# Layer 1 of a two-layer transformer block: output projection fenced behind the next scores, its addition behind the copies, and the first feed-forward input made beside the attention

## The chip, the cores and the metric

The kernel runs on one NeuronCore of one Trainium2 chip (trn2). The metric is device time in microseconds: the median of several runs. Beside it stands one execution taken with the hardware profiler, from which all rows of the trace are read.

The engines are called as the profile calls them: PE (TensorE) multiplies matrices, and PEld is its weight load; DVE (VectorE) and ACT (ScalarE) do elementwise work and read PSUM, the memory into which PE writes; POOL (GpSimd) does elementwise work on SBUF only; SP issues transfers. Each engine executes its own queue in order.

## The reference

Two layers run one after the other over 2048 tokens of 512 channels. Layer 0 has a windowed attention and a mixture of experts; the change leaves them as they are. Layer 1 is, in short:

```python
h = layernorm(x) * (1 + ca) + sa
x = x + ga * attention(h)      # 16 heads of 32, 4 key heads, window 128, 16 leading tokens always seen
h = layernorm(x) * (1 + cb) + sb
x = x + gb * ffn(h)

def attention(h):
    q, k, v = rope(h @ Wq + bq), rope(k of h @ Wkv + bkv), v of h @ Wkv + bkv
    return softmax(q @ k.T / sqrt(32), masked) @ v @ Wo + bo

def ffn(h):
    h = fwht(h * SU_ug) / 64
    h = silu(h @ W_gate.T * s_gate) * (h @ W_up.T * s_up)
    h = fwht(h * SU_dp) / 64
    return h @ W_down.T * s_down
```

`fwht` is the normalised Walsh-Hadamard transform over the last axis: 512 for the input, 2048 for the second. Everything is float32.

## The kernel before, in words

The 2048 tokens are 16 tiles of 128 rows; `x_sb` holds them all in SBUF through the whole kernel. The code is one program in Python that unrolls every loop. It states an order of instructions; a planner then writes the queue of each engine. The planner walks through the program in a timeline of its own, with estimated durations: an engine that is free takes, of the instructions that it believes ready, the one that stands earliest in the code. So an instruction from far below can be pulled ahead into a gap (the statistics `st_f`, `mv_f` of the feed-forward input are done tile by tile within the attention), and two instructions can come out in another order than the code has them. The real durations play no part in that order; semaphores see to it that it is safe. `tc.issue_after(ins)` fixes one thing: instructions made in its block stand behind `ins` in the queue of its engine. It makes no engine wait for another.

A buffer is a tile of a pool: tiles of one tag share `bufs` places, and a tile has to wait until its place is free. A pool that is opened after another was closed uses the same space again, and its first writers wait for the last readers of the old tiles.

**Layer 1's attention** (pools from L1052 on). Its work is cut in units `(i, jp)`: tile `i` and half of the heads, 32 units. `scores(i, jp)` makes 32 small matmuls into four PSUM banks (tag `s`, `bufs=4`, so one unit fills all four); for each of its eight head groups DVE reduces the scores with mask and maximum (`ng`, `nb`, L1096) and ACT makes the exponentials with their sum (`pr`, L1106). Keys for a tile are gathered by POOL (`kw`, L1062). `turn(i, jp)` transposes the probabilities on PE (`pt`, L1124, two banks with tag `t`, four transposes to a bank) and copies them to SBUF (`pts`, L1125), on DVE for the first 128 keys and on ACT for the others. `values(i)` multiplies by the values (`o`), spreads the reciprocal sums over the channels by 16 small products (`rd`), and DVE makes `oTs` from both (L1151, L1152). `out1(i)` multiplies by `wo` (`po`, eight matmuls of 512 columns; it uses the same PSUM bank as `rd`) and returns the addition to `x_sb` (L1159) as a step for later.

The loop runs over step `a`: the scores of unit `a`; the addition that is waiting; `values` of the tile whose second half was unit `a-2`; `turn` of unit `a-1`; and at once `out1` of that tile. So the projection is in the code ahead of the scores of step `a+1`, and its addition behind them.

**The feed-forward part** (from L1178). Opening its pools places the weights `wug` (64 KB a partition) and `wd` in the space that the attention used; 16 transfers of 512 KB for `wug`, on SP and ACT in turns, and four of 1 MB for `wd` follow (L1186, L1188). `ffn_in(g)` makes the input of four tiles: statistics, `xn_f` (L229), transposes `nT_f` (L243), their eviction with scale and shift into `hT` (L245 on ACT, L247 on DVE), two stages of butterflies over the four chunks of channels (L1200, L1201: on DVE for `g = 0`, on POOL for the others), and a product with the 128x128 Hadamard matrix (`xh`), copied out by ACT (L1207). Then, for each of 16 chunks `f` of the inner channels, come `gate` and `up` (eight matmuls of 512 columns each), SiLU on ACT (`sg`, L1229), the product on DVE (`act`, L1231), and `y` for the chunk before. `gate` and `up` have one PSUM bank each.

All matmuls carry line L129, which is the helper `mm`; they are told apart by tile name.

Of the kernel before, what the change touches and what calls it, by code (L numbers as in the profile page):

```python
# [22 lines left out]
P = 128  # L23
T = 2048
NT = T // P
D = 512
# [97 lines left out]
def block_kernel(ctx: ExitStack, tc: tile.TileContext, t: dict, out: bass.AP):  # L124
# [90 lines left out]

    def normed(tiles, pool, tag):
        n = len(tiles)
        mv = small.tile([P, n, 2], F32, tag="mv", name=f"mv_{tag}_{tiles[0]}")
        for a, i in enumerate(tiles):
            st = small.tile([P, 6], F32, tag="st", name=f"st_{tag}_{i}")  # L220
            V.bn_stats(st, x_sb[:, i, :])
            V.bn_aggr(mv[:, a, :], st)
        rs = small.tile([P, n], F32, tag="rs", name=f"rs_{tag}_{tiles[0]}")
        S.activation(rs, mv[:, :, 1], AF.Sqrt, bias=eps)
        V.reciprocal(rs, rs)
        got = []
        for a, i in enumerate(tiles):
            xn = pool.tile([P, D], F32, tag="xn", name=f"xn_{tag}_{i}")
            V.tensor_scalar(xn, x_sb[:, i, :], mv[:, a, 0:1], rs[:, a : a + 1], ALU.subtract, ALU.mult)  # L229
            got.append(xn)  # L230
        return got

    def normed_T(tiles, hT, c0, scale, shift, pool, psum, tag, ptag="ps", keep=None):
# [6 lines left out]
        for c in range(KC):  # L240
# [5 lines left out]
            else:  # L246
                V.tensor_scalar(hT[:, c, c0 : c0 + n], ps[:, :n], scale[:, c : c + 1], shift[:, c : c + 1], ALU.mult, ALU.add)  # L247

    modp = ctx.enter_context(tc.tile_pool(name="modp", bufs=1))
# [234 lines left out]
    su_dp = load(l1, "L1_su_dp", [P, FC])  # L484
    ws_dp = load_row(l1, "L1_ws_dp", D)
    bo1 = load_row(l1, "L1_bo", D)
# [485 lines left out]
    with tc.tile_pool(name="a1", bufs=1) as ap:  # L972
# [10 lines left out]
        with tc.tile_pool(name="b1", bufs=1) as bp, tc.tile_pool(name="b1h", bufs=2) as hp, tc.tile_pool(  # L983
# [8 lines left out]
            for g in range(NT // 4):  # L992
# [51 lines left out]
                if g == 0:  # L1044
                    nc.sync.dma_start(
                        out=v2[64:80, :, :, :].rearrange("p i a m -> p (i a) m"), in_=bc(va[0:16, 0, :], 1, 2 * NT)
                    )

        with tc.tile_pool(name="s1", bufs=2) as sp, tc.tile_pool(name="q_s", bufs=4, space=PSUM) as p_s, tc.tile_pool(
            name="q_t", bufs=2, space=PSUM  # L1050
# [3 lines left out]
            W = P + 64  # L1054
            keys, prs, pts_, outs, totals = {}, {}, {}, {}, {}

# [9 lines left out]
            def scores(i, jp):  # L1066
# [9 lines left out]
                for cp in range(2):  # L1076
# [3 lines left out]
                    for c2 in range(2):  # L1080
                        for a in range(2):
                            for j, s in ss.items():
                                r = slice(32 * j, 32 * j + 32)
                                q0 = i * P + 64 * a
                                mm(
                                    s[64 * a : 64 * a + 64, c2, 0:nk],
# [3 lines left out]
                    for c2 in range(2):  # L1090
                        for j, s in ss.items():
                            c = 2 * cp + c2

                            nb = small.tile([P, 1], F32, tag="nb", name=f"nb_{i}_{c}_{j}", bufs=6)
                            ng = sp.tile([P, W + 16], F32, tag="ng", name=f"ng_{i}_{c}_{j}", bufs=4)
                            V.tensor_tensor_reduce(  # L1096
# [17 lines left out]
            def turn(i, jp):  # L1114
# [3 lines left out]
                for j in (2 * jp, 2 * jp + 1):  # L1118
                    pr = prs.pop((i, j))
                    for b in range(1 if i == 0 else 2):  # L1120
                        n = 80 if b else P
                        pt = p_t.tile([P, 4, P], F32, tag="t", name=f"pt1_{i}_{j}_{b}")
                        for c in range(4):
                            TE.transpose(pt[0:n, c, :], pr[:, c, b * P : b * P + n], ident)  # L1124
                        (S.copy if b else V.tensor_copy)(  # L1125
                            pts_[i][0:n, b, j, :], pt[0:n].rearrange("p c q -> p (c q)")
                        )

            def values(i):
# [17 lines left out]
                for c in range(4):  # L1147
                    for j in range(4):
                        mm(rd[32 * j : 32 * j + 32, c, :], rs[:, c, j : j + 1].to_broadcast([P, HD]), ident)
                outs[i] = sp.tile([P, 4, P], F32, tag="oTs", name=f"oTs_{i}")  # L1150
                S.copy(outs[i], o)  # L1151
                V.tensor_tensor(outs[i], outs[i], rd, ALU.mult)  # L1152

            def out1(i):
# [4 lines left out]
                return lambda: V.tensor_tensor(x_sb[:, i, :], x_sb[:, i, :], po, ALU.add)  # L1159

            units = [(i, jp) for i in range(NT) for jp in range(2)]
            add = None
            for a in range(len(units) + 3):
                if a < len(units):
                    scores(*units[a])
                if add is not None:
                    add()
                    add = None
                done = units[a - 2][0] if 2 <= a < len(units) + 2 and units[a - 2][1] == 1 else None
                if done is not None:  # L1170
                    values(done)
                if 1 <= a <= len(units):
                    turn(*units[a - 1])
                if done is not None:
                    add = out1(done)


    with tc.tile_pool(name="f1", bufs=1) as fp, tc.tile_pool(name="f1n", bufs=5) as np_, tc.tile_pool(  # L1178
# [11 lines left out]
        def ffn_in(g):  # L1190
            hT = hp.tile([P, KC, D], F32, tag="hT", name=f"hT2_{g}", bufs=1)
            normed_T(list(range(4 * g, 4 * g + 4)), hT, 0, sc, sh, np_, p_t, "f1")
            xh = hp.tile([P, KC, D], F32, tag="xh", name=f"xh_{g}")
            src, dst = hT, xh
            h = 1
            while h < KC:
                a = src.rearrange("p (n two h) m -> p n two (h m)", two=2, h=h)
                b = dst.rearrange("p (n two h) m -> p n two (h m)", two=2, h=h)
                eng = G if g else V
                eng.tensor_tensor(b[:, :, 0, :], a[:, :, 0, :], a[:, :, 1, :], ALU.add)  # L1200
                eng.tensor_tensor(b[:, :, 1, :], a[:, :, 0, :], a[:, :, 1, :], ALU.subtract)  # L1201
                src, dst = dst, src
                h *= 2
            for c in range(KC):
                ps = p_t.tile([P, D], F32, tag="ps", name=f"xh_{g}_{c}")
                mm(ps, had, src[:, c, :])
                S.copy(xh[:, c, :], ps)  # L1207
            return xh

        xh = ffn_in(0)  # L1210
        for g in range(NT // 4):
# [95 lines left out]
```

## Time and profile before

| what | us |
|---|---|
| median of 3 runs (2305.62 to 2310.59) | 2306.02 |
| the profiled execution's own time | 2301.6 |
| its span (first to last instruction) | 2299.8 |
| PE busy in the span | 2122.3 |
| PE weight loads | 1178.8 |
| DVE busy | 847.7 |
| ACT busy | 473.6 |
| POOL busy | 559.0 |
| layer 1: end of the first output projection | 1331.3 |
| layer 1: end of the last output projection | 1578.0 |
| layer 1: start of the first gate matmul | 1601.5 |

Busy times are sums over the whole span and hide stages with different limits, and the ends of matmuls are modelled, so that a busy PE need not be doing all that it could. A row of the trace's groups reads "line, engine, operation, output <- inputs, shapes, count | busy us, mean ns of one | idle time ahead of it and what ended it". A row of waits reads "waiting engine, tile and line <- what ended the wait: us in total, times, longest". The chain is the work that ended last, followed back from the end: each piece with its start, its duration, engine, tile and line.

### The profile page before, as it was taken

To read this page: it belongs to the slowest core of one execution; us is meant where nothing else is said; L and a number is where in the kernel's file an instruction comes from. 1 tells how busy PE (TensorE), PEld (TensorE's weight loads), DVE (VectorE), ACT (ScalarE), POOL (GpSimd) and SP (SyncE) were. 2 spreads that over 40 slices of the span, in tenths; PEclk is the share of its full clock that TensorE was granted. 3 is DMA by queue.
4 is the path that set the end of the run, shared out by engine and by line. 5 is a ranking of instruction groups with operands and counts; after the bars stand their busy time and mean duration, and the time that the engine had idled before them with its cause. 6 is when DMAs were issued, how large, how long until landed. Compare 5 with 4: busy or idle time off the path is not lost.

```text
span 2299.8 us, 27707 instructions
## 1 busy us (share of the span) xinstructions
PE 2122.3 (92%) x10584; PEld 1178.8 (51%) x10584; DVE 847.7 (37%) x2177; ACT 473.6 (21%) x1114; POOL 559.0 (24%) x444
## 2 busy tenths in 40 slices
PE   3999978999999999999639999997999999999999
PEld 3665645545555566676315555554444444444444
DVE  3246655154544433345366456554011011000101
ACT  0124413111111111111001356653010010010000
POOL 2300000365665666654424100000010010010000
PEclk9899975799999999999869899998999999999999
DMA  9800113589899899999752000005000000000000
GB/s 355 299 2 19 38 58 110 166 200 224 220 236 235 208 244 239 253 301 313 163 195 59 19 2 1 2 2 218 2 0 19 0 0 4 15 0 0 19 0 19
DMA packets 137350, 256.40 MB, mean 111 GB/s; under 512 B 52649, under 2 KB 55657, under 8 KB 134657
## 3 DMA queue, kind: packets, MB, share of 16 engines
q1 hardware_dynamic: 95136, 159.48, 20.9%
q0 software_dynamic: 36032, 77.30, 16.2%
q10 hardware_dynamic: 6048, 17.83, 2.1%
q8 instruction: 85, 1.39, 0.2%
q14 instruction: 49, 0.39, 0.1%
HBM read 180.56 MB, written 71.65 MB: 110 GB/s over the span
## 4 chain that ended last, share of the span: by engine, by line
PE 81%; DVE 6%; DMA 6%; ACT 4%; issue 1%; POOL 1%; ACTq 0%; POOLq 0%; SPq 0%; DVEq 0%
PE y L129 18%; PE gu L129 10%; PE up L129 9%; PE gate L129 9%; PE gub L129 5%; PE xp L734 3%; PE q L129 3%; ACT pr L1106 3%; PE s L129 3%; PE po L129 2%; PE mod L129 2%; PE po_a L129 2%; DMA sum<-yo,tidx 2%; PE o L129 2%; PE pt L1124 2%; PE tps L129 2%
## 5 line engine op out<-in xcount | busy, mean ns | idle before, releaser
L793 POOL DMA_INDIRECT sum<-yo,tidx x164 | 268.7, 1638 | 120.6 <-DMA sum<-yo,tidx 36.5
L507 POOL DMA_INDIRECT xring<-h_d,tidx x164 | 168.0, 1025 | 510.9 <-DVE tidx L687 331.3
L1231 DVE SCALAR_TENSOR_TENSOR act<-up,L_ws_up,sg 128x512 f32<-128x512 f32 x64 | 48.1, 751 | 598.6 <-PE up L129 598.6
L129 PE MATMUL gu<-xT,w 128*128 128x312 f32 (+26 forms) x1024 | 245.5, 398 | 6.6 <-DVE xT L739 6.6
L129 PE MATMUL gate<-xh,wug 128*128 128x512 f32 x512 | 230.7, 592 | 0.0
L129 PE MATMUL up<-xh,wug 128*128 128x512 f32 x512 | 230.7, 592 | 0.0
L129 PE MATMUL y<-wd,act 128*128 128x512 f32 x512 | 229.5, 592 | 0.0
L129 PEld LDWEIGHTS gu<-xT,w 128*128 128x128 f32 x1024 | 191.7, 192 | 60.7 <-issue 16.5
L1229 ACT ACTIVATE sg<-gate,L_ws_gate 128x512 f32<-128x512 f32 x64 | 44.0, 687 | 575.4 <-PE gate L129 575.4
L129 PEld LDWEIGHTS up<-xh,wug 128*128 128x128 f32 x512 | 97.3, 190 | 122.5 <-issue 122.5
L129 PEld LDWEIGHTS y<-wd,act 128*128 128x128 f32 x512 | 97.3, 190 | 122.5 <-issue 122.5
L129 PEld LDWEIGHTS gate<-xh,wug 128*128 128x128 f32 x512 | 96.8, 190 | 119.6 <-issue 119.6
L129 PE MATMUL y<-w,hA 128*128 128x512 f32 (+22 forms) x328 | 148.8, 596 | 0.9 <-DVE yo L789 0.9
L789 DVE SCALAR_TENSOR_TENSOR yo<-y,wc,modr 128x512 f32<-128x512 f32 (+22 forms) x164 | 117.1, 745 | 80.1 <-PE y L129 68.4
L737 ACT ACTIVATE xT<-xp,modc,modc 128x312 f32<-128x312 f32 (+26 forms) x128 | 74.3, 580 | 316.0 <-PE xp L734 286.3
L1200 POOL TENSOR_TENSOR xh<-hT 128x1024 f32<-128x1024 f32 x3 | 7.6, 2524 | 503.3 <-DVE xn_f L229 335.9
L1106 ACT ACTIVATE pr<-ng,nb 128x208 f32<-128x208 f32 (+1 forms) x256 | 115.4, 453 | 55.1 <-DVE nb L1096 55.1
L129 PE MATMUL gub<-xT,w 128*64 128x312 f32 (+26 forms) x1024 | 125.4, 398 | 0.0
L734 PEld LDWEIGHTS xp<-cst,xring 128*128 128x128 f32 x656 | 72.3, 141 | 68.1 <-issue 46.6
L734 PE MATMUL xp<-cst,xring 128*128 128x128 f32 x656 | 98.3, 282 | 1.9 <-DVE xT L739 1.2
L755 DVE TENSOR_TENSOR hA<-hA,gu 128x312 f32<-128x312 f32 (+26 forms) x64 | 28.2, 440 | 186.7 <-PE xp L734 99.6
L129 PEld LDWEIGHTS gub<-xT,w 128*64 128x64 f32 x1024 | 70.5, 137 | 44.8 <-issue 11.3
(311 smaller groups left out, 2662.6 us busy)
## 6 DMA issues: line engine op xcount, KB each, us to landing
w<-in_L_gu SPq DMA_DIRECT2D x64, 768.0 KB, 7.3
sum<-xring SPq DMA_DIRECT2D x5, 4352.0 KB, 21.9
w<-in_L_dn SPq DMA_DIRECT2D x64, 256.0 KB, 8.3
wm<-in_L_wmod SPq DMA_DIRECT2D x9, 1024.0 KB, 6.8
w<-in_L_dn SPq DMA_DIRECT2D x64, 128.0 KB, 8.7
sa<-sum SPq DMA_DIRECT2D x32, 256.0 KB, 9.0
h_d<-xn_f SPq DMA_DIRECT2D x16, 256.0 KB, 2.9
wda<-in_L_Wdown SPq DMA_DIRECT2D x8, 512.0 KB, 13.9
```

The lines of the kernel that those rows point to most:

```text
L129: return TE.matmul(o, lhsT, rhs, start=start, stop=stop)
L507: return G.indirect_dma_start(out=dst, out_offset=None, in_=src[:, :], in_offset=bass.IndirectOffsetOnAxis(ap=idx, axis=0))
L734: st_["pe"] = TE.transpose(xp[:, b * P : (b + 1) * P], xg[:, c * P : (c + 1) * P], ident)
L737: S.activation(xT[:, c, 0:n], xp[:, 0:n], AF.Identity, bias=sh, scale=sc)
L755: V.tensor_tensor(o[:, 0:n], o[:, 0:n], ps[1][:, 0:n], ALU.mult)
L789: V.scalar_tensor_tensor(yo, ys[h], shares[h][rows, b : b + 1], m0[5][rows, :], ALU.mult, ALU.mult)
L793: G.indirect_dma_start(out=sums[k][:, :], out_offset=bass.IndirectOffsetOnAxis(ap=idx, axis=0), in_=yo, in_offset=None, compute_op=ALU.add,)
L1106: S.activation(prs[i, j][:, c, :nk], ng[:, :nk], AF.Exp, bias=nb, scale=-1.0, accum_out=totals[i][:, c, j : j + 1],)
L1124: TE.transpose(pt[0:n, c, :], pr[:, c, b * P : b * P + n], ident)
L1200: eng.tensor_tensor(b[:, :, 0, :], a[:, :, 0, :], a[:, :, 1, :], ALU.add)
L1229: S.activation(sg, pg, AF.Silu, scale=wsg[:, f : f + 1])
L1231: V.scalar_tensor_tensor(acts[f], pu, wsu[:, f : f + 1], sg, ALU.mult, ALU.mult)
```

## The change

- In step `a` of the attention's loop the projection no longer follows `turn`. It is written one step later, behind the scores of that step, and fenced on PE behind the last score matmul (`behind["PE"]`). Its addition is written behind `turn` of that later step, fenced on DVE behind the last copy of transposed probabilities there (`behind["DVE"]`).
- The input of the first four tiles of the feed-forward part (`hT0`, `xh0`) is made in a generator `ahead()`. From step 16 on, one piece of it follows each step: the statistics; one tile at a time its `xn`, its transposes into one bank of tag `t` and four evictions of 128x128; the butterflies, on POOL; two empty pieces; and one Hadamard product with its copy at a time. Its tiles lie in a pool `fx` of their own on the other side of SBUF. The feed-forward part then starts with `xh0`.
- To make room, `ng` has three buffers in place of four, `oTs` one in place of two, and the row `ws_dp` lies in a pool that is closed before layer 1.
- The butterflies become a function, always on POOL; `normed` is cut in two (`moments` and the rest).

```diff
-    def normed(tiles, pool, tag):
+    def moments(tiles, tag):
         n = len(tiles)
...
         V.reciprocal(rs, rs)
+        return mv, rs
+
+    def normed(tiles, pool, tag):
+        mv, rs = moments(tiles, tag)
...
+    def butterflies(eng, src, dst):
+
+        h = 1
+        while h < KC:
+            a = src.rearrange("p (n two h) m -> p n two (h m)", two=2, h=h)
+            b = dst.rearrange("p (n two h) m -> p n two (h m)", two=2, h=h)
+            eng.tensor_tensor(b[:, :, 0, :], a[:, :, 0, :], a[:, :, 1, :], ALU.add)
+            eng.tensor_tensor(b[:, :, 1, :], a[:, :, 0, :], a[:, :, 1, :], ALU.subtract)
+            src, dst = dst, src
+            h *= 2
...
-    ws_dp = load_row(l1, "L1_ws_dp", D)
+    ws_dp = load_row(rp, "L1_ws_dp", D)
...
+        fx = ctx.enter_context(tc.tile_pool(name="fx", bufs=1, side="right"))
...
-                                mm(
+                                behind["PE"] = mm(
                                     s[64 * a : 64 * a + 64, c2, 0:nk],
...
-                            ng = sp.tile([P, W + 16], F32, tag="ng", name=f"ng_{i}_{c}_{j}", bufs=4)
+                            ng = sp.tile([P, W + 16], F32, tag="ng", name=f"ng_{i}_{c}_{j}", bufs=3)
...
-                        (S.copy if b else V.tensor_copy)(
+                        copied = (S.copy if b else V.tensor_copy)(
                             pts_[i][0:n, b, j, :], pt[0:n].rearrange("p c q -> p (c q)")
                         )
+                        if b == 0:
+                            behind["DVE"] = copied
...
-                outs[i] = sp.tile([P, 4, P], F32, tag="oTs", name=f"oTs_{i}")
+                outs[i] = sp.tile([P, 4, P], F32, tag="oTs", name=f"oTs_{i}", bufs=1)
...
+            hT0 = fx.tile([P, KC, D], F32, tag="hT", name="hT2_0")
+            xh0 = fx.tile([P, KC, D], F32, tag="xh", name="xh_0")
+
+            def ahead():
+                mv, rs = moments([0, 1, 2, 3], "f1")
+                yield
+                for i in range(4):
+                    xn = fx.tile([P, D], F32, tag="xn", name=f"xn_f1_{i}")
+                    V.tensor_scalar(xn, x_sb[:, i, :], mv[:, i, 0:1], rs[:, i : i + 1], ALU.subtract, ALU.mult)
+                    ps = p_t.tile([P, KC, P], F32, tag="t", name=f"nT_f1_{i}")
+                    for c in range(KC):
+                        TE.transpose(ps[:, c, :], xn[:, c * P : (c + 1) * P], ident)
+                    for c in range(KC):
+                        o = hT0[:, c, i * P : (i + 1) * P]
+                        if c % 2:
+                            S.activation(o, ps[:, c, :], AF.Identity, bias=sh[:, c : c + 1], scale=sc[:, c : c + 1])
+                        else:
+                            V.tensor_scalar(o, ps[:, c, :], sc[:, c : c + 1], sh[:, c : c + 1], ALU.mult, ALU.add)
+                    yield
+                butterflies(G, hT0, xh0)
+                yield
+                yield
+                for c in range(KC):
+                    ps = p_t.tile([P, D], F32, tag="t", name=f"xh_0_{c}")
+                    mm(ps, had, hT0[:, c, :])
+                    S.copy(xh0[:, c, :], ps)
+                    yield
+
             units = [(i, jp) for i in range(NT) for jp in range(2)]
-            add = None
+            pending = None
+            side = ahead()
             for a in range(len(units) + 3):
                 if a < len(units):
                     scores(*units[a])
-                if add is not None:
-                    add()
-                    add = None
+
+                add = None
+                if pending is not None:
+                    with tc.issue_after(behind["PE"].ins):
+                        add = out1(pending)
+                    pending = None
                 done = units[a - 2][0] if 2 <= a < len(units) + 2 and units[a - 2][1] == 1 else None
                 if done is not None:
                     values(done)
+                    pending = done
                 if 1 <= a <= len(units):
                     turn(*units[a - 1])
-                if done is not None:
-                    add = out1(done)
+                if add is not None:
+                    with tc.issue_after(behind["DVE"].ins):
+                        add()
+                if a >= 16:
+                    next(side, None)
+            for _ in side:
+                pass
...
-            hT = hp.tile([P, KC, D], F32, tag="hT", name=f"hT2_{g}", bufs=1)
+            hT = fx.tile([P, KC, D], F32, tag="hT", name=f"hT2_{g}")
...
-            xh = hp.tile([P, KC, D], F32, tag="xh", name=f"xh_{g}")
...
-                eng = G if g else V
...
+            xh = (hp if g % 2 else fx).tile([P, KC, D], F32, tag="xh", name=f"xh_{g}", bufs=1)
+            butterflies(G, hT, xh)
...
-        xh = ffn_in(0)
+        xh = xh0
```

More of the change, by code (lines that the diff above doesn't have):

```diff
@@ L1054, in block_kernel @@
             W = P + 64
-            keys, prs, pts_, outs, totals = {}, {}, {}, {}, {}
+            keys, prs, pts_, outs, totals, behind = {}, {}, {}, {}, {}, {}
             def window(i):
@@ L1190, in ffn_in @@
         def ffn_in(g):
-            hT = hp.tile([P, KC, D], F32, tag="hT", name=f"hT2_{g}", bufs=1)
+            hT = fx.tile([P, KC, D], F32, tag="hT", name=f"hT2_{g}")
             normed_T(list(range(4 * g, 4 * g + 4)), hT, 0, sc, sh, np_, p_t, "f1")
-            xh = hp.tile([P, KC, D], F32, tag="xh", name=f"xh_{g}")
[L1194 to L1198, printed above, removed]
-                eng = G if g else V
[L1200 to L1203, printed above, removed]
+            xh = (hp if g % 2 else fx).tile([P, KC, D], F32, tag="xh", name=f"xh_{g}", bufs=1)
+            butterflies(G, hT, xh)
             for c in range(KC):
                 ps = p_t.tile([P, D], F32, tag="ps", name=f"xh_{g}_{c}")
-                mm(ps, had, src[:, c, :])
+                mm(ps, had, hT[:, c, :])
                 S.copy(xh[:, c, :], ps)
             return xh
-        xh = ffn_in(0)
+        xh = xh0
         for g in range(NT // 4):
```

## The prediction

> **What bounds the kernel now.** The page comes first: PE is busy 92% of the span and holds 81% of the chain that ended last. That average hides the two places that the change touches, so next comes the chain in order of time over layer 1's attention. One tile of it:
>
> ```profile
> 1438.22 0.85 PE s L129 x12
> 1439.07 1.87 PE o L129 x32
> 1440.94 0.88 PE rd L129 x32
> 1441.81 1.02 PE pt L1124 x8
> 1443.34 1.03 PE pt L1124 x8
> 1444.36 3.45 PE po L129 x8
> 1447.83 0.70 DVE x_sb L1159
> 1448.56 0.69 DVE st_f L221
> 1450.00 3.35 ACT pr L1106 x15
> ```
>
> The end of a tile hangs together in series: the projection `po` (PE), its addition (DVE), then the statistics, and only behind these the next reductions `ng` and exponentials `pr`. The waits of the same stage (1320 to 1560 us: total, times, longest) say who pays:
>
> ```profile
> ACT pr L1106 <- DVE nb L1096: 52.3, 19, 4.6
> DVE x_sb L1159 <- PE po L129: 40.3, 14, 3.7
> ```
>
> DVE stands with the addition at the head of its queue until `po` has ended; the reductions behind it wait, and ACT behind them. Afterwards PE pays: from the end of `po` to the first `o` (1447.8 to 1455.8) it has only 60 scores and 16 transposes, 5.4 us of work, in 8.0 us. A table of windows (span, busy PE, PEld, DVE, ACT, POOL, clock, DMA) shows a whole stage, an ordinary tile, and one in three times a slower one:
>
> ```profile
> 1331.30:1567.70 236.40, 225.59 (x2344) 138.26 (x2345) 141.44 (x577) 148.32 (x527) 9.52 (x36) 0.96 0.01 2
> 1415.30:1431.50 16.20, 15.52 (x170) 9.77 (x167) 9.94 (x41) 9.93 (x37) 0.79 (x3) 1.00 0.01 2
> 1447.80:1467.00 19.20, 18.52 (x170) 10.60 (x171) 10.14 (x42) 11.74 (x39) 0.79 (x3) 0.82 0.01 2
> ```
>
> From the end of the first `po` to that of the fifteenth are 14 tiles, 16.89 us each. DVE and ACT need about 10 us of that; neither is a bound. PE's busy 15.5 is no measure, as matmul ends are modelled, so I add its work from rows where it runs dense: 64 scores at 0.0555 (28 in 1.55 us) 3.55, 32 transposes at 0.128 4.08, `o` 1.87, `rd` 0.88, `po` 3.45: 13.8 us. The tile at clock 0.82 ran `o` and `rd` in 5.2 us instead of 2.8, right after the quiet 8 us; three of the 14 did, some 9 us in all.
>
> The second place is the boundary to the feed-forward part, in the chain from 1574 us:
>
> ```profile
> 1574.29 3.71 PE po L129 x8
> ...
> 1578.92 10.49 DMA wug<-in_L_Wug
> 1589.41 0.02 issue
> 1589.43 0.34 ACTq L1186
> 1589.77 0.05 issue
> 1589.82 1.46 ACT hT L245 x2
> 1591.30 1.23 DVE xh L1200
> ...
> 1595.06 6.47 PE xh L129 x8
> ```
>
> The last `po` ends at 1578.0, the first `gate` starts at 1601.5: 23.5 us with 5.5 us of PE work. Its longest piece is no need for data: ACT issues eight weight transfers, stalls in them until 1589.8, and the evictions `hT` stand behind.
>
> **The change, part by part.**
>
> *Projection behind the next scores, addition behind the copies.* Nothing is removed. PE's order in a pair of units becomes: scores, `po`, 16 transposes | scores, `o`, `rd`, 16 transposes, or 7.3 and 6.6 us, where it was 3.8 and 10.0. An ACT half is eight `pr` at 0.45 plus two or three copies at 0.57, at most 5.3 us, and fits under either. Behind the fenced `po` stand 16 transposes on PE; their `pr` were done a unit earlier. Behind the fenced addition stand the next reductions on DVE, delayed by 0.7 us under 3 us of PE work. The period's floor is 13.8. Transposes have two banks, which opens 0.5 us between pairs (1442.84, now filled by four scores): 14.8 if unfilled, and I add 0.2 for waits. Taken: 15.0; ends 14.2 and 16.9 (the planner orders by its own estimates, so the gain may fail). (16.89 - 15.0) x 14 = **-26.4 us**.
>
> The skill rule that bears on the slow tiles is in "TensorE: Matmul & The Clock Gate", Part 1: an idle window of about 3.4 us halves PE's clock. The row: 0.82 after a sparse stretch that is never idle so long. By the rule as worded the sparse stretch is harmless, the slow tiles have another cause and stay (-18); by the row, which links them to sparseness, they go with it (-26). I go by the row.
>
> *Shorter buffers.* `ng` 4 to 3: DVE makes one in 0.295 us, ACT takes one in 0.45, so ACT never lacks one; DVE's last reduction of a unit ends one ACT step, 0.45, later, hidden under `po` or `o`. Without that cover it costs 0.9 a tile, 12.6 us. `oTs` 2 to 1 and `ws_dp`'s other pool: nothing, since `po` of the tile before has ended half a tile earlier, and the row is loaded in the same place of SP's queue.
>
> *The first feed-forward input beside the attention.* Moved: the statistics and the root with its two 1.28 us table loads, which already stand in the attention (the planner had pulled them ahead); 4 `xn` (0.54 on DVE); 16 transposes; their evictions, now 16 of 128x128 in place of 4 of 128x512; 4 butterflies, from DVE (1.22 each) to POOL; 8 `xh` matmuls; 4 copies (0.59 on ACT). No DMA is issued or passed. On a PE that sets the pace: 16 x 0.128 + 8 x 0.43 = 5.5 us. Evictions of 128x128 are not in the trace: between 0.17 and 0.37 on DVE (128x4, 128x208 rows), 0.30 and 0.45 on ACT; I take 0.25 and 0.35, near the larger forms, so 0.7 us for a tile with the engines side by side. Each of the eight extra users of the two transpose banks may hold PE up for 0 to 0.9 us; I take 0.4: 3 us. Sum **+8.5**; ends 4 (half of the PE work falls in gaps) and 16 (`xh` placed before POOL is done, as in the feed-forward part: 4.2 us idle and 3.0 at half clock).
>
> Against it speaks "SBUF — State Buffer", "Who interferes with whom": a VectorE instruction in a two-port mode and a GpSimd one exclude each other for a whole instruction. The row:
>
> ```profile
> L229 DVE TENSOR_SCALAR xn_f<-x_sb,mv_f,rs_f x4: 540/1552/2580, 1693.7 to 1697.1; 128x512 f32<-128x512 f32 x4
> ```
>
> Beside POOL's butterflies an `xn` took up to 2.58 us. By the rule alone, DVE work beside 10.1 us of butterflies (4 at 2.52) is at risk; but here the four `xn` come before the butterflies by their data, and the reductions, copies and additions read PSUM or one SBUF operand, which the rule excepts. Taken 0; 5 us at the other end. Key windows on POOL (0.8 us a tile) are made some 20 us early (at 1439.2 for scores at 1462) and stand a 10 us delay.
>
> *The boundary after.* The first transfers issue when the last `po` frees their space, as now, and landed 4.7 to 5.0 us later: `gate` 0 at +4.8, `up` 0, +11.7. `gate` 1 needs `sg` 0, which stands behind ACT's eight issues (+11.8), a table load (1.28) and itself (0.69): +13.8, a stall of 2.1. PE at half clock after its 4.8 us idle (`xh` 6.47 for 3.43) would delay `gate` 0 by up to 3; that overlaps this stall. So 6.9 us instead of 23.5: **-16.6**; ends -13 and -19.
>
> *Sum.* -26.4 + 8.5 - 16.6 = -34.5. The profiled execution took 2301.6 us (span 2299.8); the median of the three runs is 4.4 above it. 2301.6 - 34.5 + 4.4 = **2271.5 us**.
>
> **The rivals.** Each has its time from the same three terms.
>
> (B) *ACT's pace takes the wait's place.* Sixteen `pr` and six copies in the planner's order hold the period at 16.2, and only the slow tiles go: -9.7 + 8.5 - 16.6 gives 2288. For it: DVE's shorter lead and "pts" copies that stand behind eight reductions. Against: ACT is busy under 10 us in 16.2.
>
> (C) *PE saturated, side work in gaps.* Period 14.2, side work at 5: -37.7 + 5 - 16.6 gives 2257. For it: ACT and DVE have 4 us to spare. Against: table loads and two transpose banks.
>
> (D) *Slower.* `po` and `rd` share one PSUM bank. If the copies, with the addition fenced behind them, end up behind the next unit's reductions on DVE, `rd` waits for the addition: 3.45 us of `po` stay in series and 0.8 (0.69 and the handover) come on top each tile, period 17.7: +11.3 + 8.5 - 16.6 gives 2309. It decides from 0.6 us a tile ((16.6 - 8.5) / 14) upward. Against: the copies need only transposes that PE runs before the next scores.
>
> (E) *The fences change nothing* because the planner ends up where it was, and side work meets a full PE: terms cancel only by accident.
>
> **How the numbers follow.** Chances: forecast 0.55, B 0.22, C 0.12, D 0.09, E 0.02. The forecast's own range is 2261 to 2284 (period 14.5 to 15.5, and 4 us from the rest). For 8 in 10 the range reaches into C and through most of B: **2255 to 2298**, leaving out D, E and C's lower part. Under 0.2% (4.6 us) this kernel's change can't be told from none. Forecast, B and C are faster: 0.89; same 0.02; slower 0.09.
>
> **What would show it.** Right: the addition no longer waits for `po`; ACT's wait for `nb` falls from 52 us to under 25; tiles at 15.0 us with the clock at 1.00; side matmuls at about half of the attention; first `gate` 5 us after the last `po`, `gate` 1 waiting for `sg`. Wrong: tiles still over 16 us with ACT or PSUM banks in the waits (B), `rd` waiting for `x_sb` (D), or PE idle ahead of `xh` for POOL.

## The result, and the profile after

| | us |
|---|---|
| before, median of 4 runs beside the changed kernel (2301.39 to 2310.59) | 2305.82 |
| changed kernel, median of 4 runs (2273.07 to 2276.15) | 2274.12 |
| ratio, with its 95% interval | 0.9863 [0.9842, 0.9884] |
| changed kernel's profiled execution; its span | 2273.46; 2271.2 |

The kernel became 1.4% faster, 31.7 us between the medians; the forecast was 2271.5. The spans differ by 28.6 us, and a few marks in both traces say where. The marks are the first copy of a gathered key window (POOL, `kw`), the end of the last `po` (read, here and in all that follows, at the start of the addition that waits for it), the start of the second gate (`gate` 1), and the end of the span. A stage is one execution's; the ratio rests on the medians.

| stage | before | after | difference | forecast |
|---|---|---|---|---|
| start of the span to the first key window | 1303.4 | 1306.7 | +3.3 | 0 |
| first key window to the end of the last `po` | 274.6 | 264.7 | -9.9 | -17.9 |
| end of the last `po` to `gate` 1 | 30.2 | 15.6 | -14.6 | -16.6 |
| `gate` 1 to the end | 691.6 | 684.2 | -7.4 | 0 |

So the total came out right, and its terms did not: the attention gave little more than half of what was forecast, and the feed-forward part gave 7.4 us that the forecast did not have (about 1.8 of them are work that moved across the mark; see the second input below). The first row is code that the change leaves alone. Over the 13 profiles of this case its mark lies between 1303.4 and 1312.6, so it is spread between executions.

One tile of the attention after, in the chain in order of time (start, us, engine, tile, line, instructions):

```profile
1413.11 3.63 PE po L129 x8
1416.74 0.87 PE pt L1141 x8
1417.61 0.50 PE s L129 x4
1418.11 1.02 PE pt L1141 x8
1419.13 0.90 PE s L129 x14
1420.54 3.82 ACT pr L1123 x16
1424.35 0.48 ACT oTs L1170
1424.86 0.69 DVE oTs L1171
1425.55 0.61 DVE pts L1142
1426.20 0.63 PE pt L1141 x4
1426.83 1.55 PE s L129 x28
1428.39 3.63 PE po L129 x8
```

`po` is followed at once by transposes; the addition and the statistics are gone from the chain. From `po` to `po` is 15.28 us. What is left of a series lies at the end of the second half: ACT's last exponentials and its copy, then on DVE `oTs`, then `pts`, and only then the transposes that PE needs.

The waits of the same stage (1320 to 1540 us: total, times, longest):

```profile
ACT pr L1123 <- DVE nb L1113: 16.1, 24, 1.7
...
DVE rs L1164 <- ACT pr L1123: 9.9, 11, 1.0
```

In the same window before, ACT waited 47.6 us for the reductions, and DVE 37.0 us with the addition for `po`, which is not in the list any more. (The prediction's 52.3 and 40.3 are of a window 20 us longer.) The second row is not new: DVE stands with the reciprocal of the sums at the head of its queue until ACT has made the last exponential, and before this took 13.1 us in 10 waits. With the addition gone, it is what stands ahead of the copies.

The table of windows (window, its length, busy PE, PEld, DVE, ACT, POOL, granted clock, share of DMA, GB/s) for 14 tiles, the one slow tile, and an ordinary one:

```profile
1336.30:1561.20 224.90, 213.89 (x2347) 131.35 (x2345) 147.40 (x573) 153.07 (x523) 18.80 (x40) 0.98 0.01 2
1384.80:1404.10 19.30, 18.06 (x176) 10.49 (x172) 11.04 (x45) 13.10 (x41) 0.79 (x3) 0.82 0.01 2
...
1413.10:1428.40 15.30, 14.70 (x170) 9.25 (x169) 10.33 (x44) 10.26 (x38) 0.79 (x3) 1.00 0.01 1
```

The 14 tiles took 224.9 us where they took 236.4; six of them now carry side work. The ordinary one is 0.9 us shorter than before (16.2), and one tile at clock 0.82 is left of three.

The boundary after, PE's timeline (start, us, line, operation, tiles, shapes, instructions, and in brackets the idle time ahead and what ended it):

```profile
1567.67 3.70 PE L129 MATMUL po<-L_Wo,oTs 128*128 128x512 f32 x8 [0.85 <-DVE oTs L1171]
1572.70 1.72 PE L247 MATMUL nT_f<-cst,xn_f 128*128 128x128 f32 x8 [1.33 <-DVE xn_f L233]
1576.37 5.40 PE L129 MATMUL gate<-xh,wug 128*128 128x512 f32 x8 [1.96 <-DMA wug<-in_L_Wug]
1581.60 3.60 PE L129 MATMUL up<-xh,wug 128*128 128x512 f32 x8
1585.04 0.60 PE L247 MATMUL nT_f<-cst,xn_f 128*128 128x128 f32 x4
1586.54 0.66 PE L247 MATMUL nT_f<-cst,xn_f 128*128 128x128 f32 x4 [0.91 <-DVE hT L251]
```

The first gate waits for nothing but its weights, 5.0 us after the last `po`. The transposes `nT_f` around it belong to the second feed-forward input (tiles 4 to 7). They were in the middle of the first group's chunks before; the planner has pulled them into this gap.

### The profile page after: what moved, and what is told of

The parts are those of the page before. It is cut to its first block, busy times and chain, and to the rows that moved or that the text cites. A ratio compares the mean times of both kernels' runs of the same rounds, so it can differ in the third digit from the quotient of the medians.

```text
span 2271.2 us, 27760 instructions
## 1 busy us (share of the span) xinstructions
PE 2103.9 (93%) x10584; PEld 1167.8 (51%) x10584; DVE 845.0 (37%) x2179; ACT 479.6 (21%) x1121; POOL 571.4 (25%) x448
## 4 chain that ended last, share of the span: by engine, by line
PE 84%; DVE 6%; DMA 5%; ACT 3%; issue 1%; POOL 1%; ACTq 0%; POOLq 0%; DVEq 0%
PE y L129 19%; PE gu L129 10%; PE gate L129 10%; PE up L129 10%; PE gub L129 5%; PE s L129 4%; PE xp L749 4%; PE q L129 3%; PE po L129 3%; PE mod L129 3%; ACT pr L1123 2%; PE po_a L129 2%; PE pt L1141 2%; PE tps L129 2%; DMA wm<-in_L_wmod 2%; DMA sum<-yo,tidx 1%
## 5 line engine op out<-in xcount | busy, mean ns | idle before, releaser
L129 PEld LDWEIGHTS gu<-xT,w 128*128 128x128 f32 x1024 | 191.4, 191 | 59.3 <-issue 16.7
L1113 DVE CUSTOM_DVE_ANT_0 ng<-s,cst 128x208 f32<-128x208 f32 (+1 forms) x256 | 87.2, 367 | 32.2 <-PE s L129 17.1
```

Source lines behind the costliest of these rows:

```text
L129: return TE.matmul(o, lhsT, rhs, start=start, stop=stop)
L1113: V.tensor_tensor_reduce(out=ng[:, :nk], in0=s[:, c2, :nk], in1=mask, scale=-SCALE, scalar=3e38, op0=ALU.add, op1=ALU.min, accum_out=nb,)
```

## Experiments

The theory to test was the forecast's: three terms, each from its own edit, that add up. The rivals were that the fences do nothing beyond the place in the code, that the shorter buffers cost something, that the slow tiles follow from sparseness alone, and for the 7.4 us in the feed-forward part that they come from the place of the `xh` products and not from the clock. The kernels below ran in three later groups, each with its own runs of the kernel before (medians 2308.56, 2307.92 and 2306.64); a ratio is to those of its own group. All of these kernels compute all that the reference does.

### The projection's new place alone, the side work alone, buffers, fences

The projection and its addition moved, with their fences, on the kernel before:

```diff
+                if pending is not None:
+                    with tc.issue_after(behind["PE"].ins):
+                        add = out1(pending)
...
+                if add is not None:
+                    with tc.issue_after(behind["DVE"].ins):
+                        add()
```

> The kernel before with the projection and its addition moved and fenced alone; buffers as before, no side work, feed-forward input where it was. Theory T (the move takes the projection and its addition out of DVE's and ACT's way; the side work and the boundary are separate terms): an ordinary tile falls from 16.2 to about 15.3 us and slow tiles become fewer, so -16 to -22 us, about 2286; the boundary stays at 23.5 us and the feed-forward part as it was. Rival B (ACT's pace takes the wait's place): at most -6, 2300 or more. Rival D (rd behind the addition): slower than before.

The side work alone is the changed kernel with the loop of before:

```diff
-                    with tc.issue_after(behind["PE"].ins):
-                        add = out1(pending)
+                if add is not None:
+                    add()
...
+                if done is not None:
+                    add = out1(done)
```

> The changed kernel with projection and addition back where they were: the first feed-forward input beside the attention, short buffers, butterflies on POOL. Theory T: the boundary gives about -15 and the second input, which now falls into the boundary, about -7 in the feed-forward part; the side work costs +3 to +9 in the attention: 2287 to 2294. Rival (PE has room in the old order, so the side work is free): 2282 to 2285. Rival (evictions behind the waiting addition stall the transposes): 2298 or more.

The moved projection with the shorter buffers:

```diff
-name=f"ng_{i}_{c}_{j}", bufs=4)
+name=f"ng_{i}_{c}_{j}", bufs=3)
...
-name=f"oTs_{i}")
+name=f"oTs_{i}", bufs=1)
```

> The moved and fenced projection with ng on three and oTs on one buffer, nothing else. Theory T (DVE still leads ACT, and the later last reduction is hidden): the same as the fences alone within 3 us. Rival (without cover, 0.45 us a unit): 6 to 13 us slower than the fences alone.

The changed kernel with everything in its new place and neither fence:

```diff
-                    with tc.issue_after(behind["PE"].ins):
-                        add = out1(pending)
+                    add = out1(pending)
...
-                    with tc.issue_after(behind["DVE"].ins):
-                        add()
+                    add()
```

> The changed kernel with both fences taken out; the projection stays in the code behind the next scores and the addition behind the copies. If the fences carry the gain, the planner puts projection and addition back and it takes 2290 or more. If the place in the code carries it, it is within 4 us of the changed kernel, 2270 to 2278.

Measured, with the stages from the profiles (attention from the first key window to the end of the last `po`, then to the first `up`, then to the end):

| kernel | median us | ratio | attention | to `up` | rest |
|---|---|---|---|---|---|
| before | | | 274.6 | 26.8 | 695.0 |
| changed | 2274.12 | 0.9863 [0.9842, 0.9884] | 264.7 | 10.2 | 689.6 |
| moved, fenced | 2290.65 | 0.9927 [0.9902, 0.9952] | 262.4 | 26.0 | 694.6 |
| side work alone | 2290.25 | 0.9924 [0.9907, 0.9940] | 285.2 | 10.3 | 689.4 |
| moved, short buffers | 2286.74 | 0.9907 [0.9887, 0.9927] | 257.2 | 25.5 | 695.3 |
| changed, no fences | 2271.61 | 0.9838 [0.9820, 0.9855] | 264.3 | 10.2 | 689.5 |

The edits add up. The moved projection changes the attention alone (-12.2, -17.4 with short buffers); the side work costs the attention 10.6 us (3 to 9 were expected) and gives the other two stages 16.5 and 5.6. The two kernels' gains by median, 17.9 and 18.3, sum to 36 us against the changed kernel's 32 to 37 (it was measured again, below).

The shorter buffers cost nothing that shows: the kernel with them is 3.9 us faster than the one without, and the profiles put that on two slow tiles fewer (one in place of three). The fences are not needed for the gain: without them the median is the same within its interval, and PE's queue is nearly the same. It is the place in the code that carries the gain; with the projection behind the scores the planner's own choice comes out almost where the fences would put it. Almost, since an ordinary tile takes 15.72 us without the fences and 15.28 with them. That the attentions come out alike here (264.3 and 264.7 us) is because no tile is slow in the profile without fences and one is in the other.

### The second input's `xh` products

In the trace after, the feed-forward part has three further inputs. Groups of PE's timeline for the second and the third:

```profile
1669.44 3.73 PE L129 MATMUL xh<-hT,cst 128*128 128x512 f32 x8
...
1849.07 2.73 PE L129 MATMUL xh<-hT,cst 128*128 128x512 f32 x4 [4.19 <-POOL hT L259]
1851.99 2.76 PE L129 MATMUL xh<-hT,cst 128*128 128x512 f32 x4 [0.19 <-ACT xh L1256]
```

and the second before:

```profile
1701.95 2.69 PE L129 MATMUL xh<-hT,cst 128*128 128x512 f32 x4 [4.25 <-POOL hT L1200]
1704.88 2.78 PE L129 MATMUL xh<-hT,cst 128*128 128x512 f32 x4 [0.24 <-ACT xh L1207]
```

Before, PE reached `xh` ahead of POOL's butterflies, idled 4.25 us and then ran the products in 5.5 us in place of 3.7. After, the second input was begun at the boundary, its butterflies ran at 1588, and its `xh` finds them done; the third and fourth still wait. If that is the source of the 7.4 us, writing the products four chunks later must give the others the same:

```diff
             butterflies(G, hT, xh)
-            for c in range(KC):
+
+            def rest(after):
+                with tc.issue_after(after.ins):
+                    for c in range(KC):
...
+            return rest
...
                 if f == FC // 2 and g + 1 < NT // 4:
-                    nxt = ffn_in(g + 1)
+                    rest = ffn_in(g + 1)
+                if f == FC // 2 + 4 and g + 1 < NT // 4:
+                    nxt = rest(fed)
```

(`fed` is the last `up` product of that chunk.)

> The changed kernel with the Hadamard products of the later three feed-forward inputs written four chunks later and fenced on PE behind that chunk's last up matmul, so that POOL has time for its butterflies. Theory P (the 7.4 us that the feed-forward part won for its second group are a wait of PE for POOL plus the half clock after it): the third and fourth group win the same, 6 to 7 us each, 12 to 14 in all against the changed kernel, about 2261. Rival (the 7.4 us come from the tiles' new place in memory or from transfers): no change, 2274.

Measured 2257.2 us, 0.9774 [0.9751, 0.9796]. All three inputs look alike now:

```profile
1709.21 3.74 PE L129 MATMUL xh<-hT,cst 128*128 128x512 f32 x8
```

The products at 1879.34 and 2049.46 also take 3.74 with no wait. From the first `up` to the end the kernel needs 676.4 us in place of 689.6: 13.2 for two inputs, 6.6 each. That is what a wait and the slow products behind it cost. (The median fell by 16.9 us where 12 to 14 were expected; no tile of this execution's attention is slow, which makes it 3.5 us shorter.)

The 7.4 us are made of three parts. The second input's wait and products took 4.25 and 5.7 us before and take 3.7 now: 6.2 us, close to the 6.6. Its 16 transposes, about 1.8 us, stood behind `gate` 1 and now stand ahead of it, so that the boundary pays for them: they are moved, not won. And the products of the third and fourth input took 0.7 us more in this execution (12.4 us in place of 11.7).

### DVE's queue at the end of a tile

Where do an ordinary tile's 15.28 us come from, when PE's rows, placed end to end, need 14.4? The queue of DVE around 1425 us after:

```profile
1424.39 0.25 DVE L1164 RECIPROCAL rs<-tot 128x16 f32<-128x16 f32 x1 [0.88 <-ACT pr L1123]
1424.86 0.69 DVE L1171 TENSOR_TENSOR oTs<-oTs,rd 128x512 f32<-128x512 f32 x1 [0.22 <-ACT oTs L1170]
1425.46 1.28 DVE L1142 COPY pts<-pt 128x512 f32<-128x512 f32 x2
```

The copies of the transposed probabilities stand behind two instructions that wait for ACT, and PE's next transposes wait for the copies, 0.9 us with the waits for ACT's copies there. If that is all, putting both instructions behind the copies brings the tile to PE's own sum:

```diff
-                V.reciprocal(rs, totals.pop(i))
+                with tc.issue_after(behind["DVE"].ins):
+                    V.reciprocal(rs, totals.pop(i))
...
-                V.tensor_tensor(outs[i], outs[i], rd, ALU.mult)
+                return lambda: V.tensor_tensor(outs[i], outs[i], rd, ALU.mult)
...
+                if done is not None:
+                    with tc.issue_after(behind["DVE"].ins):
+                        scaled()
```

(The last piece stands behind `turn`.)

> The changed kernel with the scaling oTs fenced on DVE behind the copies of the same step, and the next reciprocal behind the copies of the step before, so that the first copy of transposed probabilities no longer stands behind two waits for ACT. Theory Q (those waits hold the second pair of transposes up by 0.9 us a tile and keep an ordinary tile at 15.3 where PE's rows add up to 14.4): tiles of 14.4 to 14.7, 8 to 12 us faster than the changed kernel, about 2264. Rival (the projection then waits for oTs instead): tiles stay at 15.3 or grow, 2274 or more.

Measured 2268.78 us, 0.9830 [0.9803, 0.9856]. An ordinary tile in its table of windows:

```profile
1412.00:1426.40 14.40, 14.40 (x169) 9.19 (x170) 10.18 (x42) 10.19 (x38) 0.79 (x3) 1.00 0.01 1
```

and DVE's queue there:

```profile
1408.41 0.69 DVE L1142 COPY pts<-pt 128x512 f32<-128x512 f32 x1 [0.52 <-PE pt L1141]
1409.93 0.69 DVE L1142 COPY pts<-pt 128x512 f32<-128x512 f32 x1 [0.83 <-PE pt L1141]
1410.54 0.68 DVE L1172 TENSOR_TENSOR oTs<-oTs,rd 128x512 f32<-128x512 f32 x1
```

The tile is 14.40 us and PE busy for all of it: now DVE waits for PE and no longer PE for DVE. The attention took 254.9 us in place of 264.7; the changed kernel without a slow tile (its repetition, below) took 261.3, so 6.4 of the 9.8 us are the order's. The median fell by only 5.3 us where 8 to 12 were expected, and its interval overlaps the changed kernel's: the tiles show the gain, the total alone would not.

### The clock at the boundary

`gate` 0 took 5.40 us. The table of windows after, two microseconds a row:

```profile
1575.00:1577.00 2.00, 0.63 (x2) 0.39 (x3) 0.94 (x3) 0.00 (x0) 0.00 (x0) 1.00 1.03 428
1577.00:1579.00 2.00, 2.00 (x4) 0.77 (x3) 0.00 (x0) 0.00 (x0) 0.00 (x0) 0.53 1.02 418
1579.00:1581.00 2.00, 2.00 (x4) 0.87 (x3) 0.00 (x0) 0.00 (x0) 0.00 (x0) 0.62 1.02 416
```

In this execution the granted clock falls only after work has come back. (It is not always so: in the kernel of the two edits below it was at 0.50 from 1566.6 us on, 1.2 us before its `gate` 0 began.) Five extra products whose results are overwritten, each counted as two instructions, were to keep PE busy over the gap:

```diff
+                if g == 0 and f == 0:
+                    for k in range(5):
+                        mm(pg, had, xh[:, k % KC, :])
```

> The changed kernel with five extra products (ten matmuls of 512 columns, about 4.3 us) into the first gate bank ahead of the first gate product, whose results the real product overwrites. Theory W (the first gate product takes 5.40 us instead of 3.43 since PE idled at the boundary and its clock fell): it takes 3.43 and the kernel gains 1 to 2 us. Rival (the weights are still landing and slow it): 5.4 as before, no gain. Rival (the extra work delays it): 1 to 3 us slower.

Measured 2276.34 us, 0.9857 [0.9836, 0.9877], the same as without. It decides nothing: six of the ten instructions were placed ahead of the last `po` and four behind it, PE still waited 2.03 us for the weights, and `gate` 0 took 5.30. The three edits together (later `xh`, DVE's order, extra products):

> The three edits of these experiments together on the changed kernel. If their terms are separate, their gains add: 12 to 14 for the later products, 1 to 2 for the warm clock, 8 to 12 for the scaling, about 2250. If they share a cause (the clock), less than two thirds of that, 2257 or more.

Measured 2253.88 us, 0.9758 [0.9740, 0.9776], 20.2 us below the changed kernel where the three expectations add up to 21 to 28. Four of the extra instructions stand behind the last `po` here too, with a wait as long as before, but this time the clock held, and the gates show what the forecast had been looking for:

```profile
1571.26 3.70 PE L129 MATMUL gate<-xh,wug 128*128 128x512 f32 x8 [2.20 <-DMA wug<-in_L_Wug]
...
1580.98 3.70 PE L129 MATMUL gate<-xh,wug 128*128 128x512 f32 x8 [0.59 <-ACT sg L1290]
```

`gate` 0 at full clock, and `gate` 1 waiting for `sg` 0, which stands behind ACT's transfers. Of the 1.7 us won on `gate` 0 about 0.7 are left at `gate` 1 (14.9 us after the last `po` against 15.6). Without the extra products:

> The changed kernel with the later products and the scaling behind the copies, without the extra products at the boundary. If the gains of the two are separate: 2274 - 17 - 6 (their own measured differences), about 2252; if the extra products of the combined kernel were worth their cost, 2256 or more.

Measured 2252.42 us, 0.9755 [0.9740, 0.9769]: the extra products are worth nothing that can be seen, and the gains of the other two edits add up (16.9 and 5.3 by median, 21.7 together).

### Half of the first chunk's weights early

The last wait at the boundary is for weights. The place of `xn` in the pool `fx` is free once the side work has made its transposes; the gate half of the first chunk is loaded there in the attention. In addition all transfers of `wug` go to SP, so that ACT is free for `sg` (the copy on DVE puts the gate half where the later groups of tiles read it):

```diff
+                first.append(fx.tile([P, D], F32, tag="xn", name="wg0"))
+                nc.sync.dma_start(out=first[0].rearrange("p (k m) -> p k m", k=KC), in_=t["L1_Wug"][:, 0, 1])
                 butterflies(G, hT0, xh0)
...
-            (nc.sync if c % 2 else nc.scalar).dma_start(out=wug[:, c], in_=t["L1_Wug"][:, c])
+            if c:
+                nc.sync.dma_start(out=wug[:, c], in_=t["L1_Wug"][:, c])
+            else:
+                nc.sync.dma_start(out=wug[:, 0, 0], in_=t["L1_Wug"][:, 0, 0])
+                V.tensor_copy(wug[:, 0, 1], first[0].rearrange("p (k m) -> p k m", k=KC))
...
+                    w = first[0][:, k * P : (k + 1) * P] if g + f == 0 else wug[:, f, 1, k, :]
```

> The kernel of the two edits, with the first gate weights (256 KB) loaded during the attention into the freed xn tile, and all sixteen weight transfers on SP, so that ACT issues none. Theory L (the boundary's rest is the landing of the first chunk, 5 us, and then the first gate product at half clock): the first gate product moves ahead of the boundary, the second starts about 11 us after the last projection instead of 15.6, and the kernel takes 4 to 5 us less than with the two edits, about 2248. Rival (one queue lands the weights later, or PE at half clock takes it back): no gain, 2252 or more.

PE's timeline at its boundary:

```profile
1570.29 1.02 PE L129 MATMUL gate<-xh,wg 128*128 128x512 f32 x2
...
1573.26 3.70 PE L129 MATMUL up<-xh,wug 128*128 128x512 f32 x8
1576.80 3.60 PE L129 MATMUL gate<-xh,wug 128*128 128x512 f32 x8
```

Products of `gate` 0 now stand on both sides of the last `po`, and `gate` 1 starts 6.3 us after it, where about 11 were expected and the kernel that this one is built on has 16.7 (its `gate` 0 took 6.48 at the low clock). Measured 2243.18 us, 0.9720 [0.9707, 0.9733]: 9.2 us below that kernel, where 4 to 5 were expected, and the fastest of this study. It beats the changed kernel, measured beside it, by 1.2%. The edit has two parts, the early half and the free ACT; no run takes them apart, so what each is worth stays open.

### The changed kernel again

Unaltered, to see what one execution's details are worth:

> The changed kernel once more, unaltered, on the chip of the two others: 2271 to 2277. Of its tiles: if the tile of 19.3 us comes from a place in the code, it stands at the same tile again; if it comes from where PE's sparse stretch falls in time, another tile or none is slow.

Measured 2270.08 us (2266.5 to 2274.96), 0.9839 [0.9823, 0.9854]. The slow tile of the first trace is not slow here. PE's timeline after:

```profile
1391.62 0.66 PE L1141 MATMUL pt<-cst,pr 128*128 128x128 f32 x4 [1.24 <-DVE pts L1142]
...
1393.66 2.35 PE L129 MATMUL s<-kw,qT 32*64 32x208 f32 x22
1395.94 5.51 PE L129 MATMUL po<-L_Wo,oTs 128*128 128x512 f32 x8
```

and the same tile in the repetition:

```profile
1391.85 0.66 PE L1141 MATMUL pt<-cst,pr 128*128 128x128 f32 x4 [1.24 <-DVE pts L1142]
...
1393.49 1.28 PE L129 MATMUL s<-kw,qT 32*64 32x208 f32 x22
1394.70 3.70 PE L129 MATMUL po<-L_Wo,oTs 128*128 128x512 f32 x8
```

The same queue, the same wait of 1.24 us to the last digit, and then scores and `po` in 7.8 us or in 4.9. The tile is 19.3 us long in the one and 16.0 in the other. The table of windows, cut where the clock changes, of the first trace:

```profile
1389.38:1392.79 3.41, 2.17 (x20) 1.14 (x19) 2.40 (x6) 2.92 (x6) 0.00 (x0) 1.00 0.00 0
1392.79:1396.21 3.42, 3.42 (x27) 1.99 (x28) 1.43 (x7) 1.67 (x2) 0.00 (x0) 0.50 0.00 0
```

and of the repetition:

```profile
1392.78:1396.19 3.41, 3.41 (x32) 1.95 (x31) 1.66 (x8) 2.19 (x3) 0.00 (x0) 1.00 0.00 0
```

The traces say what sets the two apart. In each of the 13 profiles all changes of the granted clock lie a whole multiple of 3.41 us from one another, and between them it is 1.00 or 0.50 (here 0.50 for 6.8 us, until 1399.62). The stretch of queue shown here, with a wait of 1.14 to 1.24 us, occurs ten times in the profiles: three times each with the moved projection and with the short buffers, once each in the changed kernel, its repetition, the later `xh` and the extra products. The end of the wait, counted from the last of these instants that are 3.41 us apart:

| end of the wait, us after that instant | tile |
|---|---|
| 1.71, 1.75, 1.78, 1.86, 2.24, 2.28 | slow, all six |
| 2.49, 2.53, 2.80, 2.93 | not slow, all four |

So the place of the wait between these instants separates the ten. No run moved it on purpose, and it holds for this stretch alone. Without the fences the wait (1.16 us) stands between other matmuls, and no tile is slow wherever it ends; and before the change the clock fell at 1453.9 us although PE had waited no more than 0.43 us at a time in the 3.4 us ahead of it.

## Why the prediction was right, and where its steps were not

The time was right because errors of opposite sign nearly cancelled, and that is luck. The attention's term was too large by 8.0 us, the boundary's by 2.0, and 3.3 went to the start of the span; the feed-forward part gave 7.4 that no step had. That makes the span 5.9 us longer than forecast. The 4.4 us by which the median was put above the profiled execution turned out 0.7, which takes 3.7 back, and the time outside the span grew by 0.5 (from 1.8 to 2.3): 2271.5 + 5.9 - 3.7 + 0.5 = 2274.2.

**Projection and addition** (forecast -26.4; sizes wrong, mechanism right). The chain, the waits and the first of the experiments agree that the series of `po`, addition and reductions is gone. The mis-sized term is the gain over 14 tiles. They gained 11.5 us with the side work in them, so 20.3 without its 8.8; the ends of the stage lost another 1.6. The move by itself gave the whole attention 12.2 us, and 17.4 with the short buffers and two slow tiles fewer. Two sizes were off:

- The floor of a period was put at 13.8 by adding rows; the kernel in which PE never waits (DVE's order) shows 14.4. Nearly all of the 0.6 lies in the two groups of four scores that stand between transposes. Each takes 0.50 us to the start of what follows, with no idle time marked, where four at 0.0555 make 0.22 (rows below); why, no run shows. The 0.5 us between pairs of transposes, added for two banks, was not the reason for the rest: that was DVE's queue, 0.9 us a tile, which the step did not have. It looked at what stands behind the fenced `po` and addition, not at what stands ahead of the copies. With a floor 0.6 too low and waits 0.3 too high, 15.0 came close to the ordinary 15.28.
- The tile that is not ordinary. The sum gave all 14 tiles 15.0; the trace has a slow one at 19.3, 4.0 us more than its neighbours. 14 times 0.28 is another 3.9: the missing 6.1, with some tiles below the ordinary length.

```profile
1416.33 0.57 PE L129 MATMUL s<-kw,qT 32*64 32x208 f32 x4
1416.83 1.09 PE L1141 MATMUL pt<-cst,pr 128*128 128x128 f32 x8
```

**Slow tiles.** I chose the row (sparse work brings a lower clock) over the rule in "TensorE: Matmul & The Clock Gate", Part 1 (an idle window of about 3.4 us), and expected them to vanish. Neither forecasts what was seen. Slow tiles came after a PE wait of 1.24 us, far below 3.4; but the repetition has the same wait and no slow tile. Counted over the 14 tiles of each profile, the stretches at clock 0.50 are: three before, three with the moved projection, one with short buffers as well, three with the side work alone, one in the changed kernel, none in its repetition, without fences, with the later `xh` or with DVE's order, one with the extra products, and one in each of the three kernels that combine edits. So they became rarer, yet they cannot be booked as removed by an order of work. Of the ten places with the same stretch of queue and the same wait, six are slow, and where the wait ends between the instants 3.41 us apart at which the clock changes goes with the outcome in all ten (above). That this is the cause fits all ten; no run tested it.

**Shorter buffers** (0): right, by the third kernel. **Side work** (forecast +8.5): right. The six tiles with side work took 100.5 us, 8.8 more than six ordinary ones; in the old order it cost 10.6. The evictions of 128x128, for which there was no row, take 0.41 us on DVE and 0.46 on ACT, above the 0.25 and 0.35 taken and, for both, just above the upper ends. The exclusion of VectorE and GpSimd of "SBUF — State Buffer", taken at 0, cost nothing that can be seen: the four `xn` (0.54 us each) came before the butterflies, these took 2.38 us each, and the 13 reductions beside them took 0.37 us each, as the others do.

**The boundary** (forecast -16.6, measured -14.6 to `gate` 1). `gate` 0 at +5.0 was right (forecast +4.8). The stall of `gate` 1 for `sg` did not appear, and something else took its place. `gate` 0 ran at the low clock, 2.0 us longer, and two groups of four transposes of the second input, with a wait of 0.91, stand ahead of `gate` 1, another 2.0. ACT's queue has the predicted shape:

```profile
1571.45 11.55 ACTq L1244 DMA_DIRECT2D wug<-in_L_Wug  x8
1583.03 1.28 ACT L1278 ACT_TABLE_LOAD   x1 [16.46 <-DMA wug<-in_L_Wug]
1584.32 0.69 ACT L1278 ACTIVATE sg<-gate,L_ws_gate 128x512 f32<-128x512 f32 x1
```

`sg` is done at 1585.0, 13.6 us after the last `po` (forecast 13.8), two microseconds before `gate` 1 comes to it. With PE at full clock, `gate` 1 did wait for it (0.59 us).

**The step that was missing.** I asked what follows the boundary's missing stall only as far as `gate` 1. The planner fills any gap with the earliest instruction that it believes ready, and the new gap behind the last `po` was filled with the second input's transposes, so that its butterflies run from 1588 on, 80 us before PE comes to its `xh`. The forecast named exactly this cost (4.2 us idle and 3.0 at a low clock) for the side input and did not ask which of the other inputs would be freed of it.

**The rivals.** B (ACT's pace) is not seen: its wait for reductions fell and the ordinary tiles are under 16. D is not seen: `rd` never waits for `x_sb`. C's saturated PE needed one more edit, DVE's order, and has the attention at 254.9. E is wrong as it stands, since the order did change; but half of it holds: the fences add little to the place in the code (0.4 us in an ordinary tile, nothing in the total that can be seen).

## What to carry to other kernels

Where an engine's queue is in order, ask of each consumer not only what it waits for but what stands ahead of it: two small instructions waiting for ACT held up copies for which PE was waiting, 0.9 us a tile. When an edit opens or closes a gap in code that is placed by a planner with durations of its own, look for what moves into it; work whose producer it believes faster than it is (here POOL's butterflies) should be written further away from its consumer, which gave 6.2 to 6.6 us for each of the three inputs. And check a forecast by stage and not by its total: this one hit the total with two terms wrong.

## What the runs showed of the hardware

- The clock differs for the same queue: 22 scores and `po` took 4.9 us or 7.8 after the same wait of 1.24 us. `gate` 0 took 5.30 us or 3.70 after waits of 2.03 and 2.20, in two kernels with the same extra products.
- In these profiles the granted clock changed only at instants a whole multiple of 3.41 us apart, between 1.00 and 0.50.
- At the boundary it fell after dense work had begun again (mean 1.00 from 1575 to 1577 us, 0.53 in the next two), or 1.2 us before it began, in another kernel.
- ACT was held for 11.55 us by issuing eight transfers of 512 KB, with no computation of its own in between, while all the DMA engines together moved 416 to 428 GB/s.
